# Groups of seven products in a convolution trunk: the third and fourth product exchanged, the next pair's matrices loaded by GpSimd's queue, and its sums made one product earlier

## The chip, the cores and the metric

The kernel runs on one core of one Trainium2 chip. The metric is the device time of one execution in microseconds (us); lower is better. The time quoted for a kernel is the median of several runs. One more execution was recorded by the hardware profiler, and everything that is read from the profile and the trace belongs to that one.

## The reference

The reference sends one image of 512 channels and 64x64 pixels through four layers, each with a residual connection and a group norm in front:

```python
x = x + _L0_conv_ref(_gn(x), wq, wk, wv, wo)          # distance attention, 8 heads
x = x + _L1_conv_ref(_gn(x), w_in, b_in, dw_w, ...)   # gated convolution
x = x + _L2_conv_ref(_gn(x), w_in, b_in, dw_w, ...)   # the same with other weights
x = x + _L3_conv_ref(_gn(x), w_qkv, s_qkv, ...)       # linear attention, depthwise 5x5
```

A gated layer (L1, L2) multiplies the 512 input channels by `w_in` (1024x512). The first 128 results are a gate, the other 896 go through a depthwise 7x7 convolution in seven chunks of 128 channels. The gate and the chunks are then multiplied together with two small products (`pw0`, `pw1`) in between, and `w_out` (512x512) leads back to 512 channels. L3 begins in the same way with `w_qkv` (768x512). Everything is float32.

## The kernel before

The attention layer fills the first 2190 us or so of the span. The change touches only what comes after it: the two gated layers in `_gated_convs` and the first part of `_linear_attention`.

**Groups of seven.** The products with `w_in` are made for two output chunks (a pair of matrices, 128 channels each) and two blocks of 512 pixels at a time. Written as 2x2 blocks that would be eight products of 256 input channels; the class `_Seven` does it with seven, after Winograd's form of Strassen's scheme. It needs four sums of the pair's matrices (`sums`, line 459, made on VectorE into two tiles `w_sum`) and four differences of the pixel blocks (`differences`, line 472, into `diff`). `steps` returns seven closures p1 to p7 in the order in which they are issued: p1, p5, p2, p7, p6, p3, p4. What each does on TensorE and after it:

- p1 starts a bank with the first matrix's channels 0 to 255, and ScalarE copies it out as `kept[0]` (line 1410 in L1 and L2, 1791 in L3).
- p5 starts a second bank with sum 0, and ScalarE copies it out as `kept[1]`.
- p2 goes on in the bank of p1 with the first matrix's other channels, so it may start only when the copy `kept[0]` has read that bank. The result leaves through ScalarE (line 1162, or 1421 for the gate).
- p7 starts a third bank with sum 2; VectorE adds it to `kept[1]` (line 518).
- p6 starts a fourth bank with sum 1; VectorE adds it to `kept[0]` (line 522).
- p3 goes on in the bank of p5 with sum 3, p4 in the bank of p7 with the second matrix. Their results, and `kept[1]`, leave through VectorE (lines 1169 and 1172, or 1423).

What leaves is written into a `plane` tile in SBUF and sent to DRAM (`F<-plane`, line 1151, issued on ScalarE's queue in L1 and L2). There are few plane tiles, so a later write to one waits for its transfer.

**Pairs.** In a gated layer the pairs are i = 0, 2, 4, 6, called here the first to the fourth pair, with four groups (k = 0 to 3) each. The function `group` wraps the seven steps: at step 0 the sums of the pair are made unless they exist, and after step 6 of a pair's last group `more` loads two further matrices, which ScalarE multiplies by the group norm's scale in place (line 407, four instructions for a matrix). One pool of six tiles holds matrices and sums together, so that a load waits until the tile that it gets has been read for the last time.

**Convolutions.** Between the steps of the groups stand the products of the depthwise convolution (`ps_cv`). Its input comes back from DRAM (`S<-F`, on SyncE's queue) and each of these transfers is followed by a copy in SBUF on ScalarE (`S<-S`, line 1205).

**Order.** TensorE's instructions keep the order of the program text (`keep_in_program_order`). On ScalarE, VectorE and GpSimd a scheduler chooses the order when the kernel is built, with a time model of its own; each engine then works its list strictly in that order, so an instruction that waits holds up all that stands behind it.

Of the kernel before, what the change touches and what calls it, by code (L numbers as in the profile page):

```python
# [22 lines left out]
NB = N // BLK  # L23
# [10 lines left out]
NDW = 7  # L34
# [403 lines left out]
class _Seven:  # L438
# [42 lines left out]
    def first(self, a, x, ps):  # L481
        self.multiply(ps, a[:, 0:2], [x(c, 0) for c in range(2)], True)

    def steps(self, a, b, s, t, x, bank, keep, put, early=lambda more, last: None, p1_kept=None):

        nc = self.nc
        ps, kept = {}, {}

        def add(j, w, hs, first):

            if first:
                ps[j] = bank(j)
            self.multiply(ps[j], w, hs, first)

        def p1():
            if p1_kept is not None:
                kept[0] = p1_kept
                add(0, a[:, 2:4], [x(2 + c, 0) for c in range(2)], True)  # L500
                put(0, 0, ps[0], p1_kept)
                return
            ps[0] = bank(0)
            self.first(a, x, ps[0])
            kept[0] = keep(0, ps[0])

        def p5():
            add(1, s[0], t[0], True)
            kept[1] = keep(1, ps[1])

        def p2():
            if p1_kept is None:
                add(0, a[:, 2:4], [x(2 + c, 0) for c in range(2)], False)
                put(0, 0, ps[0], None)

        def p7():
            add(2, s[2], t[2], True)
            nc.vector.tensor_add(kept[1], kept[1], ps[2])

        def p6():  # L520
            add(3, s[1], t[1], True)
            nc.vector.tensor_add(kept[0], kept[0], ps[3])
            early(kept[0], kept[1])

        def p3():
            add(1, s[3], [x(2 + c, 1) for c in range(2)], False)
            put(0, 1, ps[1], kept[0])

        def p4():
            add(2, b[:, 2:4], t[3], False)  # L530
            put(1, 0, ps[2], kept[0])
            put(1, 1, kept[1], kept[0])

        return [p1, p5, p2, p7, p6, p3, p4]


class _SevenTurned(_Seven):
# [557 lines left out]
class _PlaneConv:  # L1095
# [60 lines left out]
    def put(self, i, k, ps, more, bias, step):  # L1156


        nc = self.nc
        if more is None:  # L1160
            self.take(
                i, k, [ps], lambda d, x: nc.scalar.activation(d, x, AF.Identity, bias=bias),
                nc.scalar,
            )
            return

        def fill(d, x, y):
            if step is None:
                nc.vector.tensor_add(d, x, y)
                return  # L1170
            for n in range(self.pair):
                nc.vector.scalar_tensor_tensor(
                    d[:, n], x[:, n], step, y[:, n], ALU.add, ALU.add
                )

        self.take(i, k, [ps, more], fill, self.store)
# [133 lines left out]
def _gated_convs(ctx, tc, a, X, vcol, vall, gmask, small, new_stats, centered, stats, mv, F):  # L1310
# [4 lines left out]
    nc = tc.nc  # L1315
# [13 lines left out]
    for layer in ("L1", "L2"):  # L1329
        pre = f"{layer}_conv_"  # L1330

        def weights(name, i):
            t = w2p.tile([P, NC, P], FP, tag="w", name=f"{name}_{layer}")
            nc.sync.dma_start(out=t, in_=a[f"{layer}_{name}"][i])
            return t


        w_in = [weights("w_in", i) for i in range(4)]
# [22 lines left out]
        rstd = norm.r  # L1361
# [27 lines left out]

        def more(n):  # L1390
            while len(w_in) < n:
                w_in.append(centered.scaled(weights("w_in", len(w_in)), rstd, nc.scalar))

        def summed(i):
            t = [w2p.tile([P, NC, P], FP, tag="w", name="w_sum") for _ in range(2)]
            t = [t[n // 2][:, n % 2 * 2 : n % 2 * 2 + 2] for n in range(4)]
            wsum[i] = t
            for _ in seven.sums(nc.vector, w_in[i], w_in[i + 1], t):
                pass
# [13 lines left out]
        def put(i, k, ps, more):  # L1413
            bias = vcol(pre + "b_in", i)
            if i:
                short = i % 2 and k % 2 == 0
                pc.put(
                    i - 1, k, ps, more, bias, step_b[:, i // 2 : i // 2 + 1] if short else None
                )
            elif more is None:  # L1420
                nc.scalar.activation(G[:, ts(k, BLK)], ps, AF.Identity, bias=bias)
            else:
                nc.vector.tensor_add(G[:, ts(k, BLK)], ps, more)
# [7 lines left out]
        def group(i, k):  # L1431


            at = list(made).index((i, k))
            mine = made[i, k]
            after = made[list(made)[at + 1]] if at + 1 < len(made) else iter(())
            steps = []

            def step(n):
                if n == 0:  # L1440
                    if i not in wsum:
                        summed(i)
                    steps.extend(
                        seven.steps(
                            w_in[i], w_in[i + 1], wsum[i], diff, view(k), bank,
                            lambda j, ps: keep(i, j, ps),
                            lambda m, n, ps, more: put(i + m, 2 * k + n, ps, more),
                        )
                    )
                    for _ in mine:  # L1450
                        pass
                steps[n]()
                for _ in range({2: 2, 5: 4}.get(n, 0)):
                    next(after, None)
                if n == 0 and i == 0:
                    for b in (2 * k + 2, 2 * k + 3) if k + 1 < NB // 2 else ():
                        taken(b)
                if n == 6 and k == NB // 2 - 1:
                    more(min(i + 6, NDW + 1))

            return [(0.5, lambda n=n: step(n)) for n in range(7)]

        def gate(i, b):
# [114 lines left out]
        last = [lambda b=b, o=o: output((5, 6), b, o) for o in range(NC) for b in range(NB)]  # L1578
# [18 lines left out]
def _linear_attention(ctx, tc, a, X, vcol, vall, ident, gmask, small, centered, stats, norm, F, Z, out):  # L1597
# [5 lines left out]
    nc = tc.nc  # L1603
    pre = "L3_conv_"
    f = FORM3
# [38 lines left out]
    with ExitStack() as st:  # L1644
# [12 lines left out]
            out=s_qkv.rearrange("p i m -> p (i m)"),  # L1657
            in_=bass.AP(a["L3_s"].tensor, a["L3_s"].offset, [[0, P], [1, NQKV * P]]),
# [5 lines left out]
        def weights(i):  # L1664
            t = w2p.tile([P, NROW], FP, tag="w", name="w_qkv")[:, 0:C].rearrange(
                "p (c n) -> p c n", c=NC
            )
            nc.sync.dma_start(out=t, in_=a["L3_w_qkv"][i])
            return t
# [37 lines left out]
        rstd = norm.r  # L1707
# [35 lines left out]
        def put(i, k, ps, more=None):  # L1743

            short = i % 2 and k % 2 == 0
            pc.put(
                i, k, ps, more, vcol(pre + "b_qkv", i),
                step_b[:, i // 2 : i // 2 + 1] if short else None,
            )
# [11 lines left out]
        def summed(i):  # L1761
            ss = [kvp.tile([P, BLK], FP, tag="kv", name="w_sum") for _ in range(2)]
            ss = [
                t.rearrange("p (n c m) -> p n c m", n=2, c=2)[:, n] for t in ss for n in range(2)
            ]
            wsum[i] = ss
            for _ in seven.sums(nc.vector, w_qkv[i], w_qkv[i + 1], ss):
                pass
# [28 lines left out]
        def group(i, k, also=()):  # L1797

            steps = []

            def begin():
                steps.extend(
                    seven.steps(
                        w_qkv[i], w_qkv[i + 1], wsum[i], diff[k][0], view(k), bank,
                        lambda j, ps: keep(i, j, ps),
                        lambda m, n, ps, more: put(i + m, 2 * k + n, ps, more),
                    )
                )

            def step(n):  # L1810
                if n == 0:
                    begin()
                if n < len(also):
                    also[n]()
                steps[n]()

            return [lambda n=n: step(n) for n in range(7)]
# [77 lines left out]
        late = []  # L1895
# [193 lines left out]
        def steps(hf, q):  # L2089
            return list(blks[hf, q][2])  # L2090
# [3 lines left out]
        early = [f for q in range(4) for f in blks[0, q][3]]  # L2094
# [12 lines left out]
        for q in range(2):  # L2107
            s = steps(0, q)
            convs([(q + 1, 1)], [s[0], both(prepare(0, q + 1), s[1])] + s[2:], 1)
        s = steps(0, 2)  # L2110
        convs([(3, 1), (4, 1)], [s[0], s[1], both(prepare(0, 3), s[2]), s[3]], 1)
        s = steps(0, 3)
# [28 lines left out]
        for q in range(3):  # L2141
            s = steps(1, q)
# [9 lines left out]
        for c in range(NC):  # L2152
            t = kvp.tile([P, BLK], FP, tag="kv", name="vk")
# [6 lines left out]
        ps = []  # L2160
# [34 lines left out]
        for b in range(2):  # L2195
            rz = row_of(b, kvp, "kv", BLK)
            for o in range(NC):
                ps = product(lambda d: M[:, d, ts(o, P)], [q[b, d] for d in range(NC)])
# [10 lines left out]
        for m in range(2):  # L2209
            wa, wb = (M[:, :, ts(2 * m + n, P)] for n in range(2))  # L2210
            if m:
                t = [kvp.tile([P, BLK], FP, tag="kv", name="w_sum") for _ in range(2)]
                t = [
                    t.rearrange("p (n c m) -> p n c m", n=2, c=2)[:, n] for t in t for n in range(2)
                ]
            else:
                t = [s_qkv[:, 2 * n : 2 * n + 2] for n in range(3)]
# [226 lines left out]
```

## Time and profile before

| what | value |
|---|---|
| time, median of 5 runs | 3751.03 us (3747.8 to 3752.15) |
| the profiled execution's own time | 3750.94 us |
| its span in the trace | 3749.2 us |
| TensorE (PE) busy | 3687.8 us, 98% of the span |
| VectorE (DVE) busy | 2743.1 us, 73% |
| ScalarE (ACT) busy | 2057.9 us, 55% |
| GpSimd (POOL) busy | 181.3 us, 5% |
| mean granted TensorE clock | 0.998 |

The span is the time from the first to the last instruction of the profiled execution. A busy share is an average over stages that have different limits. The views used below are the list of waits of one engine (who waited for whom, total, number of times, longest), the timeline of one engine (start, duration, operation, number of instructions merged in the row, and in brackets the idle time before it and what ended that), the table by windows (busy time per engine, then the granted clock, the DMA share and GB/s) and the list of DMA issues (queue, number, size, median time from issue to landing). A float32 product of one group appears on TensorE as four MATMUL records, and two products that stand next to each other begin 1.72 us apart.

### The profile page before, as it was taken

The numbers are of one execution on the slowest core, as the hardware profiler recorded it, in microseconds if no ns is written. First come the engines' busy times: TensorE is split into PE (matmuls) and PEld (weight loads), VectorE is DVE, ScalarE is ACT, GpSimd is POOL, SyncE is SP. The second block draws the span as 40 slices with busy tenths as digits, with TensorE's granted clock in tenths as the row PEclk, the third lists the DMA queues.
The fourth block names the chain that finished last, engine by engine and source line by source line (L and its number), as shares of the span: only waits on it lengthen the run. The fifth ranks groups of instructions, "written<-read, shape, count | busy, mean of one in ns | idle before, by whom it ended". The sixth has DMA issues, their size and how long they took to land. (4 is left out here: it accounts for less than half of the span.)

```text
span 3749.2 us, 81704 instructions
## 1 busy us (share of the span) xinstructions
PE 3687.8 (98%) x35096; PEld 1711.1 (46%) x35096; DVE 2743.1 (73%) x3593; ACT 2057.9 (55%) x2994; POOL 181.3 (5%) x174
## 2 busy tenths in 40 slices
PE   7999999999999999999999999999999999999999
PEld 6544444444464444444333344554444544445544
DVE  6677777777766777777878767766777677766647
ACT  3577774777735777747567545662356632355210
POOL 1000000000000000010000000000000000232212
PEclk9999999999999999999999999999999999999999
DMA  2000000000000000000000016762056630574322
GB/s 102 10 7 7 4 7 12 7 4 7 7 4 10 7 7 4 7 12 7 4 4 7 4 69 186 200 191 69 20 168 192 197 102 24 155 189 122 79 70 93
DMA packets 183470, 222.73 MB, mean 59 GB/s; under 512 B 15800, under 2 KB 124600, under 8 KB 182976
## 3 DMA queue, kind: packets, MB, share of 16 engines
q1 hardware_dynamic: 158752, 158.36, 15.7%
q10 hardware_dynamic: 21312, 48.03, 3.6%
q0 software_dynamic: 3040, 11.08, 0.9%
q8 instruction: 277, 4.54, 0.5%
q14 instruction: 89, 0.73, 0.1%
HBM read 157.51 MB, written 59.90 MB: 58 GB/s over the span
## 5 line engine op out<-in xcount | busy, mean ns | idle before, releaser
L844 ACT ACTIVATE pt<-ps_s,A 128x512 f32<-128x512 f32 x2048 | 1286.3, 687 | 446.8 <-PE ps_s L836 436.7
L836 PE MATMUL ps_s<-O,K 64*64 64x512 f32 x8192 | 1419.0, 589 | 0.0
L1017 DVE TENSOR_TENSOR acc<-acc,pt 128x1024 f32<-128x1024 f32 x960 | 1177.5, 1227 | 325.0 <-ACT pt L844 299.3
L856 PE MATMUL av<-pt,O 64*64 64x512 f32 x4096 | 747.0, 589 | 0.0
L856 PE MATMUL av<-pt,V 64*64 64x512 f32 x4096 | 673.5, 589 | 0.0
L836 PEld LDWEIGHTS ps_s<-O,K 64*64 64x64 f32 x8192 | 438.1, 133 | 514.9 <-issue 464.8
L1205 ACT COPY S<-S 32x1295 f32<-32x1295 f32 (+1 forms) x272 | 341.5, 1256 | 229.8 <-DMA S<-F 120.4
L856 PEld LDWEIGHTS av<-pt,O 64*64 64x64 f32 x4096 | 238.2, 133 | 250.5 <-issue 237.7
L856 PEld LDWEIGHTS av<-pt,V 64*64 64x64 f32 x4096 | 209.2, 133 | 268.6 <-issue 254.2
L1128 PE MATMUL ps<-diff,w_sum 128*128 128x512 f32 x516 | 242.5, 602 | 4.4 <-DVE w_sum L459 3.6
L1128 PEld LDWEIGHTS ps_cv<-S,T 64*32 64x32 f32 x13824 | 193.8, 105 | 115.7 <-issue 79.8
L1128 PE MATMUL ps_cv<-S,T 64*32 64x128 f32 x13824 | 234.1, 273 | 8.7 <-issue 5.3
L1128 PE MATMUL ps<-h,w_out_L 128*128 128x512 f32 x512 | 229.6, 599 | 1.5 <-DVE X L1488 1.4
L472 DVE TENSOR_TENSOR diff<-X 128x512 f32<-128x512 f32 x200 | 133.3, 683 | 67.8 <-PE ps L1128 37.0
L400 ACT ACTIVATE X<-X,gn_less 128x512 f32<-128x512 f32 x118 | 75.2, 709 | 154.2 <-DVE gn_less L130 153.4
L1128 PE MATMUL ps<-X,w_in_L 128*128 128x512 f32 x304 | 145.7, 610 | 9.2 <-ACT kept L1410 6.0
L1128 PEld LDWEIGHTS ps<-diff,w_sum 128*128 128x128 f32 x516 | 94.8, 190 | 118.4 <-issue 106.5
L1128 PEld LDWEIGHTS ps<-h,w_out_L 128*128 128x128 f32 x512 | 94.0, 190 | 118.3 <-issue 96.5
L1128 PE MATMUL ps<-h,pw_L 128*128 128x512 f32 x320 | 144.3, 600 | 2.5 <-DVE h L1476 2.3
L1259 DVE STREAM_TRANSPOSE h<-ps_cv 128x512 f32<-128x512 f32 x112 | 109.2, 1048 | 50.5 <-PE ps_cv L1128 50.4
L472 DVE TENSOR_TENSOR diff<-X,diff 128x512 f32<-128x512 f32 x200 | 134.7, 683 | 11.1 <-PE ps L1128 11.1
L1128 PE MATMUL vkp<-kT,vT 128*128 128x512 f32 x256 | 115.2, 592 | 0.0
(284 smaller groups left out, 3355.5 us busy)
## 6 DMA issues: line engine op xcount, KB each, us to landing
T<-in_L_T_dram SPq DMA_DIRECT2D x112, 384.0 KB, 4.2
F<-plane ACTq DMA_DIRECT2D x112, 324.0 KB, 3.8
S<-F SPq DMA_DIRECT2D x224, 162.0 KB, 4.6
S<-G SPq DMA_DIRECT2D x96, 153.0 KB, 4.8
row<-G SPq DMA_DIRECT2D x48, 272.0 KB, 3.5
T<-in_L_T_dram SPq DMA_DIRECT2D x48, 256.0 KB, 4.1
G<-plane POOLq DMA_DIRECT2D x33, 289.0 KB, 2.8
rd<-R SPq DMA_DIRECT2D x64, 128.0 KB, 2.9
```

Of the source, the lines that this page charges most:

```text
L400: return self.nc.scalar.activation(xs, xs, AF.Identity, bias=less)
L472: yield eng.tensor_tensor(t[j][c], a(c), b(c), ALU.subtract)
L836: nc.tensor.matmul(ps[ts(half, D), ts(h, BLK)], K[rows, t * P + half * D : t * P + (half + 1) * D], QO[pair][rows, cols], start=True, stop ...
L844: exp = nc.scalar.activation(pt[:, ts(h, BLK)], ps[:, ts(h, BLK)], AF.Exp, bias=A[:, t, h : h + 1])
L856: nc.tensor.matmul(av[half][rows, :], v[keys, t * P + h * D : t * P + (h + 1) * D], pt[keys, ts(h, BLK)], start=(t == 0), stop=(t == NT - 1),)
L1017: add = nc.vector.tensor_add(acc, acc if u > 1 else first, pt)
L1128: self.tc.keep_in_program_order(self.nc.tensor.matmul(*args, **kw))
L1205: nc.scalar.copy(second, first)
L1259: nc.vector.transpose(out, src)
```

## The change

Three things are changed.

1. With `late=True` the steps of a group are issued as p1, p5, p7, p2, p6, p3, p4. This holds for the groups of L1, L2 and the `w_qkv` groups of L3; the later groups of L3 keep the old order.
2. The matrices that `more` loads are loaded by GpSimd's queue instead of SyncE's: four in each gated layer.
3. In the last group of a pair the sums of the next pair are asked for before step 6 (p4) instead of before step 0 of the next pair's first group.

```diff
@@ class _Seven
-    def steps(self, a, b, s, t, x, bank, keep, put, early=lambda more, last: None, p1_kept=None):
+    def steps(self, a, b, s, t, x, bank, keep, put, early=lambda more, last: None, p1_kept=None, late=False):
...
-        return [p1, p5, p2, p7, p6, p3, p4]
+        return [p1, p5, p7, p2, p6, p3, p4] if late else [p1, p5, p2, p7, p6, p3, p4]
@@ _gated_convs
-        def weights(name, i):
+        def weights(name, i, queue=nc.sync):
             t = w2p.tile([P, NC, P], FP, tag="w", name=f"{name}_{layer}")
-            nc.sync.dma_start(out=t, in_=a[f"{layer}_{name}"][i])
+            queue.dma_start(out=t, in_=a[f"{layer}_{name}"][i])
             return t
...
         def more(n):
             while len(w_in) < n:
-                w_in.append(centered.scaled(weights("w_in", len(w_in)), rstd, nc.scalar))
+                w_in.append(centered.scaled(weights("w_in", len(w_in), nc.gpsimd), rstd, nc.scalar))
...
                             lambda j, ps: keep(i, j, ps),
-                            lambda m, n, ps, more: put(i + m, 2 * k + n, ps, more),
+                            lambda m, n, ps, more: put(i + m, 2 * k + n, ps, more), late=True,
                         )
                     )
                     for _ in mine:
                         pass
+                if n == 6 and k == NB // 2 - 1 and i + 2 < NDW + 1:
+                    summed(i + 2)
                 steps[n]()
@@ _linear_attention
-                        lambda m, n, ps, more: put(i + m, 2 * k + n, ps, more),
+                        lambda m, n, ps, more: put(i + m, 2 * k + n, ps, more), late=True,
```

## The prediction

> **What bounds the kernel now.** I read the busy table first, then TensorE's list of waits, then the timelines around each wait that the change can touch, then the clock there and the DMA issues.
>
> ```profile
> PE 3687.8 (98%) x35096; PEld 1711.1 (46%) x35096; DVE 2743.1 (73%) x3593; ACT 2057.9 (55%) x2994; POOL 181.3 (5%) x174
> ```
>
> TensorE is the bound: 3749.2 - 3687.8 leaves some 61 us in which it does nothing, in the whole span. No product is added or removed, so the change is worth what it takes from, or adds to, TensorE's waits.
>
> ```profile
> PE ps L1128 <- ACT kept L1410: 6.0, 8, 1.7
> PE ps L1128 <- DVE w_sum L459: 3.6, 2, 2.0
> PE ps L1128 <- ACT kept L1791: 2.7, 1, 2.7
> PE ps L1128 <- DVE kept L518: 1.0, 1, 1.0
> ```
>
> The first and third rows are p2 waiting for the copy `kept[0]`, the second p5 waiting for a new pair's sums, the last p4 waiting for line 518. Together 13.3 us, 0.35% of the time: all that can be won, but for what a wait does to the clock afterwards. The second row is shown on TensorE's timeline (second to third pair, L1), and in the table by windows, whose last three columns are granted clock, DMA share and GB/s:
>
> ```profile
> 2311.99 1.88 PE L1128 MATMUL ps<-X,w_in_L 128*128 128x512 f32 x4
> 2315.84 2.76 PE L1128 MATMUL ps<-diff,w_sum 128*128 128x512 f32 x4 [1.97 <-DVE w_sum L459]
> 2318.39 2.85 PE L1128 MATMUL ps<-X,w_in_L 128*128 128x512 f32 x4
> ```
>
> ```profile
> 2318.00:2322.00 4.00, 4.00 (x8) 1.62 (x7) 3.61 (x6) 2.65 (x3) 0.00 (x0) 0.71 0.94 266
> ```
>
> After an idle 1.97 us the next two products take 2.76 and 2.85 instead of 1.88 us (granted clock 0.71): 1.83 us more. The waits of 1.64 us (L2) and 2.65 us (L3) had no such tail. ScalarE at the same place:
>
> ```profile
> 2310.53 1.55 ACT L407 ACTIVATE w_in_L<-w_in_L,gn_r 128x128 f32<-128x128 f32 x5
> 2316.83 0.69 ACT L1410 ACTIVATE kept<-ps,vec 128x512 f32<-128x512 f32 x1 [0.91 <-DVE w_sum L459]
> 2319.35 1.27 ACT L1205 COPY S<-S 32x1295 f32<-32x1295 f32 x1
> 2322.37 3.85 ACT L1205 COPY S<-S 32x1295 f32<-32x1295 f32 x3 [0.40 <-ACT plane L1162]
> ```
>
> To be seen: the copy `kept[0]` of the new pair comes before the S copies, and five of the eight scalings are over before it.
>
> **Part 1, the exchange.** p2 gets the 1.72 us of p7 (and often a stretch of convolution) as cover. Seven of the eight waits on line 1410 lie away from the change of pair, and each is at most 1.70 us: L1 0.22 + 0.90 + 0.83 = 1.95, L2 0.22 + 0.95 + 1.70 + 0.85 = 3.72. All go. In L3 p7 takes 1.72 of the 2.65. What is late next: p7 needs its bank and `diff` earlier. In the built order its bank is the one that the group before freed with line 1169 or 1423, and p6 takes the one freed by the last 1172; in the rows both writers end before the new starts, except in L3, where the wait of 1.05 us for line 518 moves ahead of the bias work but p5 and p7 come to stand within 0.5 us of their banks: I take 0 for it, with ends -1.0 and +1.0. No instruction is added.
>
> **Part 2, the sums.** In the built order of the changed kernel three sums stand right behind VectorE's last transpose (line 1265, which started at 2313.20) and in front of the four 1172. That moves the first sum from 2315.78 to 2314.8, so p5 still waits: nominal start 2313.4 (0.31 earlier, as the 0.31 us wait before it goes), real start 2314.8. The 1172 end at about 2316.8 instead of 2315.4, line 1169 at 2317.4. The sum instructions are the same four, 0.34 us apart, on an engine that is not the bound.
>
> **Part 3, the loads, and what the order makes of them.** The sums, asked for first, now get the tiles that fall free first. The two loads wait for the end of p3 and of p4 instead of p2 and p6, 3.4 us later each, and with them the eight scalings. SyncE loses eight issues of 0.33 us that nothing waited for; GpSimd, idle there, issues them. But the scheduler has rearranged ScalarE's list at the second change of pair, alike in L1 and L2: two issues of F, all eight scalings, three S copies, and only then `kept[0]` of the new pair, with p2 behind it. Walked through on the clock of the trace before (L1):
>
> - the second F issue needs line 1169: 2317.4, plus 0.35 = 2317.8;
> - eight scalings (four in 1.28): 2.5, so 2320.3; the loads, issued by 2311.5, have landed (even at 6.2 us);
> - three S copies in 3.85: 2324.2. Their transfers are no help: the first was issued at 2315.03 and in use at 2319.35;
> - `kept[0]` 0.69: 2324.9, so p2 starts at 2325.0. p7 ended at 2318.3. TensorE waits 6.7 us.
>
> p2, p6 and p3 take 5.3, to 2330.3; before, p3 ended at 2326.4: +3.9. In L2 the same rows stand 482.5 to 482.8 us later, p5 waits 0.7 and p2 6.7, and p3 ends at 2812.7 instead of 2807.2: +5.5. On top, a tail of slow clock: from 0 (as after 2.65 us) to 1.83 (as after 1.97). I take 1.83, since this idle is longer than both: +5.7 and +7.3 (before, L1 already paid it).
>
> The Trainium skill, "TensorE: Matmul & The Clock Gate", section "What's actually happening", says that the clock is halved after an idle window of about 3.4 us and restored after a busy one as long. By it the wait of 1.97 us should have cost no clock, which the row contradicts, while a wait of 6.7 us must; its price, an estimate from that page, would be 1.7 us each, and the sum 0.3 us lower.
>
> At the first change of pair, ScalarE's list has the second matrix's four scalings right before `kept[0]`. That matrix's load now starts when p4 ends, at 2249.2.
>
> ```profile
> w_in_L<-in_L_w_in_dram SPq DMA_DIRECT2D x16, 256.0 KB, 2.6
> bt<-in_L_w_projT_dram POOLq DMA_DIRECT2D x4, 256.0 KB, 6.2
> s_row<-in_L_sp_dram ACTq DMA_DIRECT2D x1, 256.0 KB, 5.1
> ```
>
> The loads from GpSimd took 6.2 where a load of the same size from ScalarE in the same stage took 5.1, so I take 2.6 + 1.1 = 3.7: landed 2252.9, scaled (1.28) 2254.2, copied (0.69) 2254.9. p2, now in fourth place, could start at 2254.2: a wait of 0.7 in each layer, 1.4 together. Ends: at 2.6 no wait; at 6.2 (2257.4) a wait of 3.2 each, 6.4 together.
>
> The skill's "DMA: Bandwidth & Descriptors", section "Latency and other measured facts", speaks against this part too: about 1 us to the first byte on GpSimd's path, 0.6 on the others. By that difference, an estimate, the load would take 3.0 and p2 would not wait, so the sum would be 1.4 lower.
>
> The third change of pair has no load, and its sums were not late before: nothing.
>
> **The sum**, against the profiled execution's own 3750.94 (median 3751.03, 0.1 apart): + 5.7 + 7.3 + 1.4 - 1.95 - 3.72 - 1.7 = +7.0, so 3758.0 us.
>
> **The rivals.**
>
> *The order does not bite (faster).* If `kept[0]` came by 2318.3, where p7 ends, p2 would follow at once: p3 would end at 2323.6 in L1 (-2.8) and at 2806.0 in L2 (-1.2); with 7.4 from the other copies 11.4 less: 3739.6. For it: ScalarE is busy 55% only, and all its work there is small. Against: eight scalings and three copies are 6.3 us of work behind line 1169, whatever waits or not. It decides when 6.6 us of that chain vanish. 0.16.
>
> *A wash.* The chain is shorter than walked (VectorE ahead by 1 us in each layer, -2; no clock tail, -3.7) and the loads cost nothing (-1.4): 3750.9, between 3747 and 3754. 0.20.
>
> *Late loads.* A GpSimd load takes 6.2 us alone too: 5.0 us more than in the sum, 3763, between 3760 and 3766. For it: the four loads of `bt` are the only ones of this size on that queue. Against: they ran beside stores; stores from that queue took 2.8 where ScalarE's took 2.4. 0.20.
>
> *Forecast.* 0.44, from 3754 (clock tails 0) to 3761 (1 us either way in L3, and a load of 5 us).
>
> **How the numbers follow.** The range runs from 3747 to 3766: it leaves out the first rival. 0.2% is 7.5 us, about what a measurement of this kernel can tell from no change; the bounds are 3743.5 and 3758.5. Faster: the first rival, 0.16. Same: the wash and 0.15 of the forecast, 0.35. Slower: late loads and the rest of the forecast, 0.49. The forecast is split unevenly because two of its terms, the idle of VectorE behind a late `kept[1]` and a later F transfer, were counted at nothing (hidden by 25% idle VectorE and by the convolution between the groups) and can only add.
>
> **What would show it.** In the profile after: the row "ACT kept L1410" holds two waits of over 6 us, one in each gated layer, in front of p2, and none of the seven small ones; the row "DVE w_sum" stays, shorter; ScalarE's timeline shows eight scalings, three S copies, then `kept`; the clock dips after both waits; L3's wait on line 1791 is near 1 us. It is wrong if the longest wait on line 1410 is under 3 us, or if the total of TensorE's waits falls.

## The result, and the profile after

| | before | after |
|---|---|---|
| time, median of the runs | 3750.47 us (3745.05 to 3756.03, 47 runs) | 3756.93 us (3749.66 to 3761.25, 27 runs) |
| the profiled execution's own time | 3750.94 us | 3756.4 us |
| its span | 3749.2 us | 3754.4 us |
| mean granted TensorE clock | 0.998 | 0.996 |

The changed kernel takes 1.0017 times as long as before, with a 95% interval of 1.0012 to 1.0022: slower by about 6.5 us, where 7.0 were predicted. The median of after lies 1.1 us under the predicted 3758.0.

TensorE's list of waits (total, number of times, longest) shows the whole exchange of small waits for large ones:

```profile
PE ps L1128 <- ACT kept L1410: 15.2, 4, 6.5
PE ps L1128 <- DVE w_sum L459: 2.4, 2, 1.8
PE ps L1128 <- DVE plane L1172: 0.5, 1, 0.5
```

Eight waits for `kept[0]` in the gated layers have become four: two of 6.5 and 6.4 us at the second change of pair in L1 and L2, and two of 1.6 and 0.7 us at the first. The small ones between the groups are gone, and so are both rows of L3 (2.7 on line 1791, 1.0 on line 518); a wait of 0.5 us on line 1172 is new there. The busy row has grown too, though no product was added:

```profile
PE 3691.3 (98%) x35096; PEld 1707.4 (45%) x35096; DVE 2753.9 (73%) x3593; ACT 2057.5 (55%) x2994; POOL 186.2 (5%) x182
```

Of the 3.5 us more of busy PE some 2.4 are no work, but products at a slow clock (2.0 us in L1 and 2.2 in L2, against 1.83 in L1 before). TensorE's timeline at the second change of pair in L1 shows where they lie:

```profile
2311.99 1.88 PE L1128 MATMUL ps<-X,w_in_L 128*128 128x512 f32 x4
2315.64 3.70 PE L1128 MATMUL ps<-diff,w_sum 128*128 128x512 f32 x8 [1.77 <-DVE w_sum L459]
2325.84 3.78 PE L1128 MATMUL ps<-X,w_in_L 128*128 128x512 f32 x4 [6.49 <-ACT kept L1410]
2329.41 2.02 PE L1128 MATMUL ps<-diff,w_sum 128*128 128x512 f32 x4
2331.27 1.88 PE L1128 MATMUL ps<-X,w_sum 128*128 128x512 f32 x4
```

The rows are p1, then p5 and p7 in one, p2, p6, p3. p2 waits 6.49 us and then takes twice its time. In the table by windows, for the stretch right behind the wait, the granted clock (third number from the end) is 0.54:

```profile
2326.00:2330.00 4.00, 4.00 (x6) 1.70 (x7) 1.35 (x3) 3.93 (x4) 0.00 (x0) 0.54 0.00 0
```

From the start of p2 to the start of p3 pass 5.43 us where two products stand 3.44 apart: 2.0 us lost to the slow clock (2.2 in L2). The reason for the wait is on ScalarE's timeline:

```profile
2317.67 0.97 ACTq L1151 DMA_DIRECT2D F<-plane  x2
2318.74 2.45 ACT L407 ACTIVATE w_in_L<-w_in_L,gn_r 128x128 f32<-128x128 f32 x8 [2.28 <-PE ps L1128]
2321.22 3.85 ACT L1205 COPY S<-S 32x1295 f32<-32x1295 f32 x3
2325.09 0.69 ACT L1410 ACTIVATE kept<-ps,vec 128x512 f32<-128x512 f32 x1
```

Two issues of F, eight scalings, three S copies, then the copy that p2 waits for. The bank of p1 was full from 2313.9 on; ScalarE worked almost without a gap from 2317.7 to 2325.8, but on other things first.

### The profile page after: what moved, and what is told of

The parts are those of the page before. It is cut to its first block, busy times and chain, and to the rows that moved or that the text cites. A ratio compares the mean times of both kernels' runs of the same rounds, so it can differ in the third digit from the quotient of the medians.

```text
span 3754.4 us, 81723 instructions
## 1 busy us (share of the span) xinstructions
PE 3691.3 (98%) x35096; PEld 1707.4 (45%) x35096; DVE 2753.9 (73%) x3593; ACT 2057.5 (55%) x2994; POOL 186.2 (5%) x182
```

## The experiments

The theory: the early sums alone make the two long waits, because they rearrange ScalarE's list; the exchange by itself only gains; GpSimd's queue costs little. The rivals: A, the loads on GpSimd's queue are what holds ScalarE up; B, the exchange itself costs, because p7 needs a bank earlier. The first four kernels are parts of the change; every edit below is shown against the changed kernel. The experiments ran where the kernel before took 3745.38 (the first four) and 3743.95 us (the others), some 6 us less than in the runs of before and after, so the ratios are to be read, not the microseconds; a difference given below in microseconds is the ratio's distance from 1, times the time of the kernel before. The expectations reckon from 3750.5. Brackets behind a ratio are its 95% interval.

**The exchange alone** (loads and sums as before).

```diff
-                if n == 6 and k == NB // 2 - 1 and i + 2 < NDW + 1:
-                    summed(i + 2)
...
-                w_in.append(centered.scaled(weights("w_in", len(w_in), nc.gpsimd), rstd, nc.scalar))
+                w_in.append(centered.scaled(weights("w_in", len(w_in)), rstd, nc.scalar))
```

> The exchange alone: loads on SyncE's queue and sums at the new pair's step 0, as before. Theory (the early sums rearrange ScalarE's list; the exchange itself only gains): in the built order the scalings stand where they stood before and kept[0] leads the S copies, so no wait over 6 us is left; the small waits for kept[0] go (L1 -1.9, L2 -3.7, L3 -1.7), p5 still waits for the first sum, some 0.5 us longer in L1 because line 1169 now stands ahead of the sums: 3750.5 - 7.3 + 0.5 to 1.5 = 3744 (3741 to 3747). Rival A (GpSimd's loads are what holds ScalarE up): the same here, 3744. Rival B (the exchange itself costs, p7 waiting for its bank): 3750 or more, with a new row of waits in front of p7.

Measured: 3736.55 us, ratio 0.9975 (0.9965 to 0.9986), so 9.4 us less, somewhat more than the 6.5 expected. No wait on line 1410 is left in the whole kernel, and of the one on line 1791 0.8 us. What has come instead is small: 0.5 us on line 1172 in front of one p7 in L3, which is rival B's mechanism at a twentieth of what the exchange brings. Rival B falls. The largest waits left in these stages are those for `w_sum` (2.6 in L1, 1.6 in L2).

**Exchange and early sums, loads on SyncE's queue.**

```diff
-                w_in.append(centered.scaled(weights("w_in", len(w_in), nc.gpsimd), rstd, nc.scalar))
+                w_in.append(centered.scaled(weights("w_in", len(w_in)), rstd, nc.scalar))
```

> The changed kernel with its loads back on SyncE's queue: exchange and early sums. Theory: the built list still has all eight scalings ahead of kept[0] at the second change of pair, but two S copies behind them instead of three, so the two long waits become about 6.45 - 1.28 = 5.2 us each, with the slow clock behind them; at the first change of pair the load lands about 0.7 us sooner, worth 0.7 to 1.5 over the two layers: 3756.9 - 2.6 - 1.1 = 3753.2 (3751 to 3756). Rival A (the queue): the long waits go, 3743 to 3745.

Measured: 3748.86 us, ratio 1.0006 (0.9997 to 1.0015), as expected (3753.2 against 3750.5 is 1.0007): 2.2 us more than before, which the interval does not tell from nothing, but some 12 us more than the exchange alone, which it does. ScalarE's and TensorE's timelines in L1:

```profile
2315.44 2.45 ACT L407 ACTIVATE w_in_L<-w_in_L,gn_r 128x128 f32<-128x128 f32 x8 [2.23 <-PE ps L1128]
2317.91 2.56 ACT L1205 COPY S<-S 32x1295 f32<-32x1295 f32 x2
2320.50 0.69 ACT L1410 ACTIVATE kept<-ps,vec 128x512 f32<-128x512 f32 x1
```

```profile
2321.24 3.78 PE L1128 MATMUL ps<-X,w_in_L 128*128 128x512 f32 x4 [5.14 <-ACT kept L1410]
2324.81 2.82 PE L1128 MATMUL ps<-diff,w_sum 128*128 128x512 f32 x4
2327.47 1.88 PE L1128 MATMUL ps<-X,w_sum 128*128 128x512 f32 x4
```

The long waits stay without GpSimd's queue, and each is 1.3 us shorter: one S copy (1.28) fewer in the list. So the list sets the wait to the length of single entries. The waits at the first change of pair are gone, so those belong to the queue. Rival A falls as the cause of the long waits. The queue is not without cost, though, as long as the early sums stand: the waits of 1.6 and 0.7 us, and one more S copy in each long wait. By the ratios (1.0017 with it, 1.0006 without) this is some 4 us, but these two intervals overlap.

**The early sums alone** (old order of steps, loads on SyncE's queue).

```diff
-        return [p1, p5, p7, p2, p6, p3, p4] if late else [p1, p5, p2, p7, p6, p3, p4]
+        return [p1, p5, p2, p7, p6, p3, p4]
...
-                w_in.append(centered.scaled(weights("w_in", len(w_in), nc.gpsimd), rstd, nc.scalar))
+                w_in.append(centered.scaled(weights("w_in", len(w_in)), rstd, nc.scalar))
```

(The kernel leaves `late` out at its two calls, which comes to the first of these two edits.)

> The early sums alone: old order of the steps (p2 third), loads on SyncE's queue. Theory: ScalarE's list has eight scalings and two S copies ahead of kept[0], and p2 has not even p7 as cover, so p2 waits about 6.9 us twice, p7, p6, p3 and p4 come behind it; the small waits of before stay, and at the first change of pair kept[0] comes about 1.6 us late in each layer: 3750.5 + 7 (L1) + 8 (L2) + 3 = 3768 (3762 to 3772), slower than before by 0.3 to 0.6%. Rival A (the queue alone does the harm, early sums help p5): 3750 or less.

Measured: 3764.59 us, ratio 1.0046 (1.0033 to 1.006): 17.2 us more, 17.5 expected. TensorE's list of waits:

```profile
PE ps L1128 <- ACT kept L1410: 23.7, 13, 6.9
```

Both long waits are 6.9 us, 1.7 more than with p7 in front of p2, which is what p7 covers (1.72). The exchange is worth most just where the early sums do their harm.

**Exchange and GpSimd's queue, sums at their old place.**

```diff
-                if n == 6 and k == NB // 2 - 1 and i + 2 < NDW + 1:
-                    summed(i + 2)
```

> The changed kernel without the early sums: exchange and GpSimd's queue. Theory: the list is that of the exchange alone, and the loads take some 0.7 us longer, mostly hidden: within 1.5 us of the exchange alone, 3744.5 (3742 to 3748). Rival A (the queue holds ScalarE up): near the changed kernel, 3754 to 3757, with the long waits.

Measured: 3737.69 us, ratio 0.998 (0.9971 to 0.9989), 0.0005 above the exchange alone (1.9 us; 1.1 by the medians), which the intervals do not tell from nothing. No wait for `kept[0]`. With the sums out of the way the queue's slower loads are hidden.

**The changed kernel with the scaling moved to VectorE**, one instruction for a matrix there:

```diff
-                w_in.append(centered.scaled(weights("w_in", len(w_in), nc.gpsimd), rstd, nc.scalar))
+                w_in.append(centered.scaled(weights("w_in", len(w_in), nc.gpsimd), rstd, nc.vector))
```

> The changed kernel with one thing moved: the matrices that are loaded at a change of pair are scaled by VectorE (one instruction each) instead of ScalarE (four each). In the built order ScalarE now has only the two F issues ahead of kept[0], neither scalings nor S copies. Theory: both waits of 6.4 us go, with the slow clock behind them, and kept[0] no longer stands behind a load at the first change of pair; p5's wait for the first sum (1.8 and 0.6) stays: 6.4 + 6.4 + 4.2 + 2.3 = 19 us less than the changed kernel, 13 us less than before, so a ratio of 0.9965 (0.995 to 0.998) to before. Rival (the F issues behind line 1169 or the late VectorE hold kept[0] anyway): waits of 2 to 4 us stay on line 1410, ratio 0.9985 to 1.

Measured: 3733.21 us, ratio 0.9969 (0.9957 to 0.9981). This is the changed kernel with all three of its parts, and one cause taken out. ScalarE and TensorE at the same place:

```profile
2315.80 0.97 ACTq L1151 DMA_DIRECT2D F<-plane  x2
2316.82 0.69 ACT L1410 ACTIVATE kept<-ps,vec 128x512 f32<-128x512 f32 x1 [2.22 <-PE ps L1128]
2318.47 1.27 ACT L1205 COPY S<-S 32x1295 f32<-32x1295 f32 x1 [0.96 <-DMA S<-F]
```

```profile
2313.78 3.70 PE L1128 MATMUL ps<-diff,w_sum 128*128 128x512 f32 x8 [1.17 <-DVE w_sum L459]
2317.56 1.98 PE L1128 MATMUL ps<-X,w_in_L 128*128 128x512 f32 x4
```

`kept[0]` follows the F issues at once, and p2 follows p7 without a wait, in L1 and in L2; no wait on line 1410 is left, none at the first change of pair either. That closes the case for the cause of the long waits: scalings and S copies ahead of `kept[0]`.

**The same idea with the sums one step earlier still**, loads on SyncE's queue:

```diff
-                if n == 6 and k == NB // 2 - 1 and i + 2 < NDW + 1:
+                if n == 5 and k == NB // 2 - 1 and i + 2 < NDW + 1:
...
-                w_in.append(centered.scaled(weights("w_in", len(w_in), nc.gpsimd), rstd, nc.scalar))
+                w_in.append(centered.scaled(weights("w_in", len(w_in)), rstd, nc.vector))
```

> Exchange, scaling on VectorE, loads on SyncE's queue, and the sums asked for one step earlier still, before p3: in the built order the sums now stand ahead of VectorE's last transposes, so that p5 should find its sum made. Theory: as the kernel with the scaling on VectorE, and 2.4 us of waits for w_sum less (up to 2 more where a slow clock followed): 14 to 17 us less than before, ratio 0.996 (0.9945 to 0.9975). Rival (the sums then wait for a tile that falls free late, and hold VectorE's list): the wait for w_sum stays or grows, waits for line 1476 or 1172 grow, ratio 0.998 or more.

Measured: 3732.36 us, ratio 0.9971 (0.996 to 0.9982): inside the range expected, but no better than the kernel before it. The wait for `w_sum` is gone as the theory said, and a wait for `kept[0]` has come in its place:

```profile
2312.38 3.60 PE L1128 MATMUL ps<-diff,w_sum 128*128 128x512 f32 x8
2317.41 1.98 PE L1128 MATMUL ps<-X,w_in_L 128*128 128x512 f32 x4 [1.44 <-ACT kept L1410]
```

p5 starts 1.40 us earlier than with the scaling on VectorE alone, p2 only 0.15. The next thing late is the pair of F issues (2315.70 to 2316.6) that stands ahead of `kept[0]` in ScalarE's list; the second of them waits for the write on line 1169.

**The loads asked for later**, scaling on ScalarE:

```diff
-                if n == 6 and k == NB // 2 - 1 and i + 2 < NDW + 1:
+                if n == 5 and k == NB // 2 - 1 and i + 2 < NDW + 1:
...
-                if n == 6 and k == NB // 2 - 1:
-                    more(min(i + 6, NDW + 1))
+                if n == 3 and k == 0 and i:
+                    more(min(i + 4, NDW + 1))
...
-                w_in.append(centered.scaled(weights("w_in", len(w_in), nc.gpsimd), rstd, nc.scalar))
+                w_in.append(centered.scaled(weights("w_in", len(w_in)), rstd, nc.scalar))
```

> Scaling stays on ScalarE, but the loads are asked for after p2 of the new pair's first group instead of after the old pair's p4, and the sums before p3; loads on SyncE's queue, exchange kept. In the built order five scalings stand ahead of the F issues and none behind them, no S copy ahead of kept[0] at the second change of pair; at the first one a scaling stands between kept[0] and kept[1]. Theory: no long wait for kept[0]; the same as with the scaling on VectorE within 3 us, ratio 0.9965 (0.995 to 0.9985). Rival (ScalarE waits for the load among the five scalings, so that the bias work and the F issues come late): a wait of 2 us or more for kept[0] or for h, ratio 0.9985 to 1.0005.

Measured: 3733.62 us, ratio 0.9968 (0.9957 to 0.998). Five scalings stand ahead of `kept[0]` here and cost nothing, since they run while ScalarE would wait for VectorE anyway. `kept[0]` comes at 2316.76, and p2 waits 1.5 us in L1 and 0.9 in L2, much as in the kernel before this one. The scaling may stay on ScalarE; only its place counts.

**The kernel before, again**, unchanged.

> The kernel before, once more, for a second trace: how much TensorE's waits of the class issue in front of ps_cv (5.3 us in the first trace, 3.1 in that of the changed kernel) and the waits for line 1476 (3.3 in all) differ between two executions of the same kernel, and whether the wait of about 2 us for w_sum in L1 is again followed by slow products. If these are scatter, 'issue' comes near 3 us and the time scatters by 2 to 3 us; if they belong to the order of before, both stay within 0.5 us.

Measured: 3744.98 us in the profiled execution, 1.0 from the median of the runs beside it. The class issue in front of `ps_cv` came to 5.0 us (5.3 in the first trace), so it is not mere scatter between these two executions; the waits for line 1476 came to 0.8 (2.3 in the first trace; the 3.3 in the expectation was misread). In L1:

```profile
2314.72 1.98 PE L1128 MATMUL ps<-diff,w_sum 128*128 128x512 f32 x4 [0.95 <-DVE w_sum L459]
2316.54 1.89 PE L1128 MATMUL ps<-X,w_in_L 128*128 128x512 f32 x4
```

The wait for `w_sum` is half that of the first trace, and no slow products follow. So the 1.97 us and the slow clock of 1.83 us behind it were, in the first trace, partly chance: 2.85 us that the prediction took as the fixed starting point in L1.

## Why the prediction was right

Each step is measured as the shift of TensorE's rows, after against before; together the shifts give the 5.2 us between the spans.

| step | predicted | measured | read from |
|---|---|---|---|
| first change of pair, L1 / L2 | +0.7 / +0.7 | +1.8 / +1.0 | p4 to p6: -0.77 to +1.07, and +5.78 to +6.77 |
| second change of pair, L1 | +5.7 | +6.8 | p3's end 2333.15 against 2326.39, p1 in both at 2311.99 |
| second change of pair, L2 | +7.3 | +7.8 | p3's end 2821.03 against 2807.20, less 6.07 before it |
| other waits for `kept[0]`, L1 | -1.95 | -2.0 | the rest of the layer |
| the same, L2 | -3.72 | -7.4 | the rest of the layer |
| L3's wait on line 1791 | -1.7 | -3.1 | from L2's end to the last `kept` of L3: +7.15 to +4.09 |

Before L1 begins, after lies 0.8 us ahead, and it loses 1.1 after L3's groups. Neither place is touched by the change.

*The order of ScalarE's list.* It came as read from the built order, and the walk through it held at every entry: scalings 2.45 us (2.5), S copies 3.85, `kept` 0.69, and waits of 6.49 and 6.44 us for 6.7 predicted. The start of p2 in L1 is 0.8 later than predicted, 2325.84 for 2325.0, because the second F issue ended at 2318.6 for 2317.8: VectorE's last transpose began 0.85 later than in the trace before. That is most of the 1.1 us that the step in L1 was short. One time in the walk was misread without consequence: the second load was not issued by 2311.5 but at 2312.70. At 6.2 us it would have landed about 1 us after the F issues, but no scaling waited for a load there.

*The slow clock.* Taken at 1.83 us for each long wait, measured 2.0 and 2.2. That any clock would be lost was the open point between 0 and 1.83. The choice of the full price held, but its reason, "since this idle is longer than both", is not what decides; the last section shows what does as far as the traces tell, and by it an idle time of 6.5 us was sure to cost the clock.

*The first change of pair* was sized too small in L1. The walk said: second load landed at 2252.9, scaled 2254.2, p2 waits 0.7. ScalarE's row:

```profile
2253.30 1.28 ACT L407 ACTIVATE w_in_L<-w_in_L,gn_r 128x128 f32<-128x128 f32 x4 [0.92 <-DMA w_in_L<-in_L_w_in_dram]
2254.48 0.67 ACT L1410 ACTIVATE kept<-ps,vec 128x512 f32<-128x512 f32 x1
```

p4 had ended at 2248.47 and the load was issued at 2249.05, so issue and landing took 4.8 us where 3.7 were taken, 0.6 of it before the issue began, for which the sum had nothing; in L2 it was 4.0, from 2738.22 to the scaling at 2742.19. From SyncE the same load, in the kernel with exchange and early sums, took 3.1 us from p4's end to the scaling (2248.79 to 2251.89). The rival of late loads was thus right in direction and wrong in size: 3.4 us is the median from issue to landing of the eight loads on GpSimd's queue, where the rival took 6.2.

*L2 and L3* gained more than the sum allowed. In L2 two rows fell that the sum did not hold: issue in front of `ps_cv` from 2.0 to 0.2 us and the waits for `h` from 1.3 to 0.4, 2.7 together. In the second trace of before these rows are 1.9 and 0.4, so the second is scatter and the first at least no scatter of that pair; with the exchange alone it is 1.4 in the same layer. Why it falls was not settled, and some 1 us of the 3.7 has no row of its own. In L3 the waits fell from 2.65 + 1.0 to 0.5, which is the shift of -3.1 in the table. More than the 1.72 counted for p7 went: p7's own wait of 0.5 us on line 1172 stands in front of p2 too, and the copy `kept[0]` came early enough against TensorE's rows that no wait for it is left (with the exchange alone 0.8 us is). And the prediction had put 0 on line 518, with ends of 1.0 either way; its 1.0 went, and the 0.5 on line 1172, for p7's bank, came.

So the mechanism stands as predicted, and the errors of size have both signs: +1.4 at the first changes of pair, +1.6 at the second ones, -3.7 in the rest of L2, -1.4 in L3. That the total came within 0.5 us of the median is therefore in part luck: the harm was 3.0 us larger than counted and the gain 5.1 us larger, and the starting point held 2.85 us in L1 that the second execution of before did not show. Of the signs named beforehand all but one came: two waits over 6 us in front of p2, none of the seven small ones, a shorter row for `w_sum` (2.4 for 3.6), a dip of the clock behind both long waits. Only L3's wait on line 1791 fell below the 1 us expected, to none. The rival in which the order does not bite is refuted by the two long waits; "a wash" lay 6 us under the median.

## What to carry to other kernels

A request that is moved one step earlier changes more than its own time: it takes the place, in a list that is worked strictly in order, that something else had. Read the built list of every engine at the place of the change, and count what stands between the awaited instruction and its data; here that gave 6.7 us for 6.5, on an engine 55% busy. And a change made of three parts should be run part by part: two of these (the exchange, alone or with GpSimd's queue) make the kernel faster by 0.2%, and the third costs more than they bring, though with the scaling off ScalarE's way all three together are faster by 0.3%. Whether that is more than the exchange alone brings (0.9969 and 0.9975) the intervals do not tell.

## What was unexpected in the hardware

The length of an idle time did not decide whether TensorE's clock fell, up to some 3 us. Two kernels differ only in the queue of the loads, and wait at the same place in L1 (TensorE's timelines, the exchange alone first, then with GpSimd's queue):

```profile
2315.30 5.11 PE L1128 MATMUL ps<-diff,w_sum 128*128 128x512 f32 x8 [2.56 <-DVE w_sum L459]
```

```profile
2314.73 3.70 PE L1128 MATMUL ps<-diff,w_sum 128*128 128x512 f32 x8 [2.69 <-DVE w_sum L459]
```

The granted clock from 2312 to 2318 is 0.73 in the first and 1.00 in the second:

```profile
2312.00:2318.00 6.00, 3.44 (x5) 1.17 (x4) 6.00 (x14) 3.11 (x6) 0.00 (x0) 0.73 0.68 216
```

```profile
2312.00:2318.00 6.00, 3.31 (x9) 1.60 (x9) 6.00 (x15) 3.78 (x7) 0.00 (x0) 1.00 0.76 239
```

The shorter wait of 2.56 us lost 1.5 us to the clock (5.11 instead of 3.60 for two products) and the longer one of 2.69 lost 0.1. The waits of 1.97 (slow, in the first trace) and 1.77 (not slow, in the changed kernel) are of the same kind.

What decides, as far as these traces show, is where the wait falls. From L1 on, the granted clock falls and recovers in each trace only at the marks of a grid of 3.413 us: a stretch of half clock lasts 3.41, 6.83 or 10.24 us, and two of one trace begin a whole number of steps apart (in the changed kernel at 2322.86 in L1 and 2810.96 in L2: 488.1 us, 143 steps). Here is the table by windows, cut at these marks, for the kernel before, the exchange alone, and the exchange with GpSimd's queue. The second number is the stretch's length, the third TensorE's busy time:

```profile
2313.50:2316.91 3.41, 1.44 (x4) 0.59 (x4) 3.41 (x9) 1.81 (x5) 0.00 (x0) 1.00 0.47 156
2316.91:2320.33 3.42, 3.42 (x6) 1.33 (x5) 3.42 (x8) 2.28 (x3) 0.00 (x0) 0.50 1.03 317
2320.33:2323.74 3.41, 3.41 (x9) 1.50 (x9) 2.65 (x6) 2.33 (x4) 0.00 (x0) 1.00 0.64 145
```

```profile
2311.34:2314.76 3.42, 1.40 (x4) 0.33 (x2) 3.42 (x8) 2.41 (x5) 0.00 (x0) 1.00 0.25 97
2314.76:2318.17 3.41, 2.87 (x4) 1.33 (x5) 3.34 (x8) 0.70 (x2) 0.00 (x0) 0.50 0.99 298
```

```profile
2310.33:2313.74 3.41, 1.70 (x4) 0.39 (x3) 3.41 (x9) 2.39 (x6) 0.00 (x0) 1.00 0.29 111
2313.74:2317.16 3.42, 2.43 (x6) 1.24 (x7) 3.42 (x8) 1.56 (x4) 0.00 (x0) 1.00 0.88 256
```

Before, all 1.97 us of the wait lay in one step, and the next step ran at half clock; it began when TensorE had been at work again for 1.1 us. With the exchange alone 2.0 of the 2.56 us lay in one step, with the same result. With GpSimd's queue the 2.69 us were split into 1.7 and 1.0, and no step was slow. Of the steps at full clock in the two gated layers, in all ten traces, each of the eight with 1.97 us or more of idle time was followed by a step at half clock, and none with 1.81 us or less was. This holds for these layers and their products: later in L3, with other products, half clock also followed steps with 1.5 us of idle time. What exactly is counted within a step was not tested.

Each of the six waits for `kept[0]` of 5.1 us or more lost 2.0 us or more (2.0 and 2.2 after 6.5 and 6.4 us in the changed kernel, 2.8 and 2.1 after 5.1 with the loads on SyncE, 2.5 and 2.8 after 6.9 with the early sums alone). That follows from the same rows: wherever an idle time of 6.5 us falls, at least 3.2 us of it lie in one step, and the loss is half of the time that TensorE works within slow steps. In L1 of the changed kernel these end at 2329.68, 3.84 us after p2's start at 2325.84, which makes 1.9 of the 2.0 us; in L2 it is 4.30 us, or 2.15 of 2.2. The 1.7 us that the prediction worked out as the other price is half of a single step; in all six cases between one and two slow steps were left. The Trainium skill, "TensorE: Matmul & The Clock Gate", section "What's actually happening", speaks of idle windows of about 3.4 us. The steps of 3.41 us agree with that, but a window did not have to be idle throughout: 1.97 us of it were enough here.
